# Layer 2 of a four-layer network on one core: token factors spread by TensorE, kernel weights made once at a turn's end, four patch banks, biases on ScalarE

## The chip, the core and the metric

One Trainium2 chip, of which the kernel uses one NeuronCore. Its engines run side by side and wait for each other through semaphores: TensorE (PE in the profile; its weight loads are PEld), VectorE (DVE), ScalarE (ACT), GpSimd (POOL) and SyncE (SP), whose queue issues the DMAs. SBUF is the working memory, PSUM the eight banks of 2 KB per partition that matmuls write to. The metric is the device time of one execution, in microseconds, as a median of several runs.

## The reference, cut to what matters

Four layers, each `x = x + layer(groupnorm(x))`, on 16 images of 64 x 64 tokens and 256 channels. The change lies in the end of layer 1 and in layer 2.

Layer 1 ends with a gate per token and a batch norm:

```python
xc = x * ca_gate
...
ma = xc * jax.nn.sigmoid(y)
...
sa = xc * jax.nn.sigmoid(s)
x2 = ma + sa
mean = jnp.mean(x2, axis=(0, 1, 2))
var = jnp.var(x2, axis=(0, 1, 2))
out = (x2 - mean) * lax.rsqrt(var + EPS) * bn_gamma + bn_beta
return jax.nn.relu(out)
```

The two sigmoids add up to one number per token, the token factor. Layer 2 is an involution: every token gets its own 3 x 3 kernel for each of 16 groups of 16 channels.

```python
r = jnp.einsum('bhwc,cd->bhwd', x, Wr) + br
r = jax.nn.relu((r - mean) * jax.lax.rsqrt(var + BN_EPS) * gamma + beta)
w = jnp.einsum('bhwd,dk->bhwk', r, Ws) + bs
w = w.reshape(B, H, W, G, KK)[:, :, :, :, None, :]
xi = jnp.einsum('bhwc,cf->bhwf', x, Wi) + bi
...
patches = patches.reshape(B, H, W, G, F // G, KK)
out = jnp.sum(w * patches, axis=-1)
```

Here `KK` is 9, so 144 weights per token, and one token's 256 outputs are 2304 products and their sums.

## The kernel before, in words

**Where the edited code stands.** The block that opens the pools `b_const` to `b_acc` (L826) does the end of layer 1 and the whole of layer 2. It first runs `batch_norm` (L879): 128 steps, one for each image and chunk of 512 tokens, in which TensorE spreads a row of token factors over all 128 partitions (L925: a column of the identity, broadcast, as weights, and the 128 x 512 table `held` as the moving operand) into a PSUM tile `pf`, VectorE multiplies (L933) and ScalarE squares. The results of image 0 are kept; the other images are multiplied again later.

**The pipeline of layer 2.** After that comes a loop of 148 turns (L1287 onward, `TURNS`). Four jobs run in each turn, for a chunk (image i, row chunk rc, 512 tokens) that is `LAG` = 0, 10, 18 and 28 turns behind: the end of layer 1 (`end_of_layer1`), the projection to `xi` (`projected`), the involution itself, and the centring of the result for layer 3 (`centred`). Eight turns make an image. The order of every engine's instructions is the order in which the Python code emits them (`tc.manual_schedule`); the pools decide the waits: a tile from a pool with n buffers waits for the release of the tile n allocations earlier.

One turn, in the order of the code:
- `loads(n+1)` (L1273): DMAs for the next turn, on SP's queue: `x2p`, `x2r`, and by `load_layer1` (L986) the tile `x1` (two DMAs) and the tile `pf` (two DMAs that broadcast a row of factors from DRAM over 128 partitions). Then the stores of the turn before.
- `step()` (L97) moves every running chain on by one `yield`. The chains are `norm2(i)` (L1056) and `norm3(i)` (L1237), which make the constants of a group norm over several turns; `step` is called three times a turn, at its start, in the middle (`between`) and near its end.
- `end_of_layer1` (L999): two VectorE operations (L1008), one per half of the channels, make z = (x1 - mean) * pf. The first writes a tile `z`, the second writes over `pf`. Then ScalarE's relu (L1017), GpSimd's add (L1021, x2 = z + x1), and in `between` ScalarE's squares (L1028).
- `weights(now[1], 1)` (L1124): TensorE makes the second 72 of the 144 kernel weights for 4 x 128 tokens, four products into a PSUM tile `pw` of one bank.
- `prepare` for the next chunk: `reduced2` (L1111; TensorE `pr`, ScalarE `rt`), `summed` and `evicted` (L1169, L1177) for the chunk before, and `patches` (L1134): nine groups of four transposes into a bank `pt`, each group copied out by ScalarE (L1151 `xs`). After the third group `between` runs: `weights(rt, 0)`, the squares and a `step()`.
- `residual` (L1156, `lo`), `turned` (L1201) and `statistics3`, then `projected` (L1090; TensorE `px`, ScalarE `pad`). In the turn that prepares a new image's first chunk, the projection's last chunk comes inside `patches`, before the groups that need it.
- `products(0, ...)` (L1181): VectorE multiplies patches by weights, 4608 elements per partition, from SBUF `xs` and PSUM `pw`; GpSimd sums them (L1198, L1199). `products(1, ...)` follows, whose sum VectorE makes itself (L1357).

**PSUM.** Eight banks: pool `tr` has three (for `pr`, `pt`, `px`, `pf` of the batch norm, the turned tiles and the small products of the norms, all in one rotation), `pwp` three (`pw`), `acc` two (`lo`).

**The bias.** The last step of `norm2` stands at a turn's start: after TensorE's `pm` (L1079), VectorE makes `b2` (L1085) and `bis` (L1087), ahead of that turn's z.

Of the kernel before, what the change touches and what calls it, by code (L numbers as in the profile page):

```python
# [15 lines left out]
P = 128  # L16
# [20 lines left out]
def network(ctx: ExitStack, tc: tile.TileContext, a: dict, out: bass.AP):  # L37
# [730 lines left out]
    facr = fac_d.rearrange("(i c) t -> i (c t)", i=NI)  # L768
# [57 lines left out]
    with ExitStack() as st:  # L826
# [4 lines left out]
        tr = st.enter_context(tc.tile_pool(name="b_tr", bufs=3, space=PSUM))  # L831
        pwp = st.enter_context(tc.tile_pool(name="b_pw", bufs=3, space=PSUM))
# [37 lines left out]
        loaded, stores, begun = [], [], []  # L870
        kept = {}

        def spare(pool, shape, tag):

            t = pool.tile(shape, F32, tag=tag, name="kept")
            flat = t.rearrange("p a b c -> p (a b c)")
            return flat[:, 0 : NCH * CT].rearrange("p (n h t) -> p n h t", n=NCH // 2, h=2)

        def batch_norm():  # L879
# [8 lines left out]
            held = wk.tile([P, 2, 256], F32, tag="z", name="held", bufs=1)  # L888
            held = held.rearrange("p a b -> p (a b)")[0 : NI * NCH]
# [26 lines left out]
            for k, (i, ch) in enumerate(todo):  # L916
                begin(k + 5)
                x1 = tiles.pop(k)
                pf = tr.tile([P, CT], F32, tag="tr", name="pf")
                parts = [(ch, 0, CT)]  # L920
                if not i:
                    parts = [(g * 4 + ch // 2, ch % 2 * 256, 256) for g in range(2)]
                for g, (row, c0, m) in enumerate(parts):
                    row += i * NCH
                    nc.tensor.matmul(  # L925
                        pf[:, g * m : g * m + m],
                        lhsT=ident[0 : NI * NCH, row : row + 1].broadcast_to([NI * NCH, P]),
                        rhs=held[:, c0 : c0 + m], start=True, stop=True,
                    )
                for h in range(2):  # L930
                    z = x1[:, h] if i else kept[ch][1][:, h]
                    at = slice(i * NCH + ch, i * NCH + ch + 1)
                    nc.vector.scalar_tensor_tensor(  # L933
                        z, x1[:, h], ngm1[:, i, h : h + 1], pf, ALU.add, ALU.mult,
                        accum_out=tot[:, 0, h, at],
                    )
                    sq = z if i else wk.tile([P, CT], F32, tag="sq", name="sq", bufs=1)
                    nc.scalar.activation(sq, z, AF.Square, accum_out=tot[:, 1, h, at])
# [47 lines left out]
        def load_layer1(i, rc):  # L986
            tks = [slice(g * 2048 + rc * 256, g * 2048 + rc * 256 + 256) for g in range(2)]
            load("x1", [P, 2, 2, 256], *(
                (lambda t, g=g: t[:, :, g], x1_d[i, :, :, tks[g]].rearrange("h p t -> p h t"))
                for g in range(2)  # L990
            ))
            load("pf", [P, 2, 256], *(
                (lambda t, g=g: t[:, g], facr[i, tks[g]].partition_broadcast(P)) for g in range(2)
            ))
# [4 lines left out]
        def end_of_layer1(i, rc):  # L999
# [4 lines left out]
            if i:  # L1004
                x1, pf = taken("x1"), taken("pf")
                zs = [wk.tile([P, 2, 256], F32, tag="z", name="z", bufs=1), pf]
                for h, z in enumerate(zs):
                    nc.vector.scalar_tensor_tensor(  # L1008
                        z, x1[:, h], ngm1[:, i, h : h + 1], pf, ALU.add, ALU.mult
                    )  # L1010
# [45 lines left out]
        def norm2(i):  # L1056
# [26 lines left out]
            yield  # L1083
            b2 = small.tile([64, 1], F32, tag="b2", name="b2")
            nc.vector.tensor_scalar(b2, pm[0:64, 2:3], sb2[0:64, 2:3], sb2[0:64, 1:2], ALU.mult, ALU.add)  # L1085
            bis = small.tile([P, 2], F32, tag="bis", name="bis")
            nc.vector.tensor_tensor(bis, bi, pm[:, 0:2], ALU.subtract)  # L1087
# [36 lines left out]
        def weights(rt, oh):  # L1124

            pw = pwp.tile([P, 4, 72], F32, tag="pw", name="pw")
            for r in range(4):
                nc.tensor.matmul(
                    pw[:, r], lhsT=rt[:, r * P : (r + 1) * P], rhs=ws[:, oh * 72 : oh * 72 + 72],
# [51 lines left out]
        def products(oh, pw, xs):  # L1181
            pd = pd_p.tile([P, 4, P, 9], F32, tag="pd", name="pd")
            run = xs.rearrange("p e j c -> p (e j c)")[:, oh * 9 * P : (oh + 1) * 9 * P]
            run = bass.AP(run.tensor, run.offset, [run.ap[0], [3 * C, 4], [9 * 16, 8], [9, 16], [1, 9]])
            nc.vector.tensor_tensor(  # L1185
                pd.rearrange("p r (g f) k -> p r g f k", f=16),
                run,
                pw.rearrange("p r (g k) -> p r g k", k=9).unsqueeze(3).broadcast_to(
                    [P, 4, 8, 16, 9]
                ),  # L1190
                ALU.mult,
            )
# [90 lines left out]
        with tc.manual_schedule():  # L1283
# [3 lines left out]
            for n in range(TURNS):  # L1287
# [14 lines left out]
                if inv:  # L1302
                    w1 = weights(now[1], 1)
                    x3 = wk.tile([P, 4, C], F32, tag="x3", name="x3", bufs=3)
# [7 lines left out]
                def prepare(late):  # L1312
# [7 lines left out]
                    def between():  # L1320
                        ahead.append(weights(rt, 0))
# [24 lines left out]
                if inv:  # L1346
                    pd = products(0, now[2], now[3])
# [6 lines left out]
                if inv:  # L1354
                    pd1 = products(1, w1, now[3])
                if inv:
                    nc.vector.tensor_reduce(x3[:, :, P:C], pd1, AX.X, ALU.add)  # L1357
                made = (*inv, x3, los) if inv else None
# [395 lines left out]
```

## Time and profile before

| | us |
|---|---|
| median of 3 runs | 7944.51 |
| lowest, highest | 7941.79, 7947.63 |
| profiled execution | 7971.0 |
| its span, first to last instruction | 7969.2 |
| batch statistics (first L925 to last L933) | 3164.5 to 3343.4 |
| layer 2's first and last product (L1185 starts) | 3455.9, 5599.4 |

| engine | busy us | share of the span |
|---|---|---|
| PE | 6865.4 | 86% |
| DVE | 5671.4 | 71% |
| ACT | 4934.1 | 62% |
| POOL | 3053.4 | 38% |

In the group lines of the profile, a line names the code line, the engine and operation, output and inputs, shapes, how often it ran; then busy time and mean duration in ns; then the idle time of the engine before it and who ended that. In timeline lines the first number is the start in us from the span's start and the second the duration; brackets hold idle time before. TensorE runs an fp32 matmul as two records, a transpose as one. Shares over the whole span are means over stages with different limits, so layer 2 is read by itself.

### The profile page before, as it was taken

What the parts mean: (1) busy time and instruction counts of PE and PEld (TensorE: products, weight loads), DVE (VectorE), ACT (ScalarE), POOL (GpSimd) and SP (SyncE); (2) the same over time, 40 slices, a digit from 0 to 9 for tenths busy, and PEclk for the clock granted to TensorE, in tenths of its full rate; (3) what the DMA queues carried; (4) which work ended last, traced back from release to release, by engine and by line L of the source; (5) the groups of instructions that cost most, each with busy time, mean ns of one, the idle gap of its engine ahead of it and who ended that gap; (6) DMA issues with size and microseconds to landing.
All of it is one profiled execution on the core that took longest, in us unless ns stands there. A gap on an engine that the chain in (4) does not pass through costs nothing.

```text
span 7969.2 us, 213876 instructions
## 1 busy us (share of the span) xinstructions
PE 6865.4 (86%) x88812; PEld 5137.4 (64%) x88812; DVE 5671.4 (71%) x6527; ACT 4934.1 (62%) x11456; POOL 3053.4 (38%) x2171
## 2 busy tenths in 40 slices
PE   7888888888888977689989999999788888888887
PEld 4666666666666664156666666666577777777776
DVE  6777777777777765879999999999444444444444
ACT  3555555555555554978787777776455555555554
POOL 1222222222222221168888888888222221111112
PEclk9999999999999986899999999999899999999999
DMA  7644444444443333967888888876688888888887
GB/s 216 196 149 133 138 137 133 135 135 135 134 137 112 117 103 103 327 209 264 285 282 286 270 287 275 288 265 224 209 259 260 258 255 261 256 253 258 248 257 236
DMA packets 1075308, 1689.89 MB, mean 212 GB/s; under 512 B 136273, under 2 KB 680354, under 8 KB 1073186
## 3 DMA queue, kind: packets, MB, share of 16 engines
q1 hardware_dynamic: 1074338, 1676.21, 65.4%
q8 instruction: 700, 11.47, 0.6%
q14 instruction: 270, 2.21, 0.1%
HBM read 1228.85 MB, written 469.76 MB: 213 GB/s over the span
## 4 chain that ended last, share of the span: by engine, by line
PE 46%; DVE 23%; issue 12%; ACT 8%; DMA 7%; POOL 3%; SPq 1%; DVEq 0%; POOLq 0%; ACTq 0%
PE pk L1458 13%; DVE pd L1185 9%; PE pa L1524 8%; PE pkv L270 5%; PE py L412 5%; DMA xn<-in_x 2%; PE pq L258 2%; PE pr L1425 2%; DVE x L1357 2%; PE pctx L336 2%; PE px L1097 1%; DVE mq L371 1%; ACT sq L421 1%; DVE z L1008 1%; DVE mq L378 1%
## 5 line engine op out<-in xcount | busy, mean ns | idle before, releaser
L1185 DVE TENSOR_TENSOR pd<-xs,pw 128x4608 f32<-128x4608 f32 x256 | 1256.0, 4947 | 5.5 <-POOL x L1199 5.3
L1458 PE MATMUL pk<-rt,span 64*128 64x176 f32 x12288 | 1183.6, 329 | 61.2 <-issue 55.0
L1468 ACT ACTIVATE wm<-pk,spanb 128x176 f32<-128x176 f32 x2560 | 845.8, 425 | 574.3 <-PE pk L1458 572.5
L1544 POOL TENSOR_TENSOR ex<-ex,rx 128x192 f32<-128x192 f32 (+2 forms) x768 | 436.7, 570 | 1826.5 <-DVE ex L1537 1329.4
L1198 POOL TENSOR_TENSOR pd<-pd 128x2048 f32<-128x2048 f32 (+2 forms) x384 | 1072.2, 2792 | 88.5 <-DVE pd L1185 68.4
L1458 PEld LDWEIGHTS pk<-rt,span 64*128 64x128 f32 x12288 | 973.2, 192 | 139.0 <-issue 81.3
L1537 DVE SCALAR_TENSOR_TENSOR ex<-pa,msk,ex 128x192 f32<-128x192 f32 x704 | 294.2, 418 | 1019.2 <-ACT ex L1536 951.9
L270 PE MATMUL pkv<-wq,xn 128*128 128x256 f32 x4096 | 979.3, 385 | 3.6 <-ACT va L279 2.0
L1524 PE MATMUL pa<-wm,xw 126*32 126x48 f32 x45056 | 751.1, 214 | 213.8 <-issue 201.0
L1473 DVE TENSOR_TENSOR wm<-pk,spanb 128x704 f32<-128x704 f32 x896 | 794.0, 888 | 192.0 <-PE pk L1458 188.8
L270 PEld LDWEIGHTS pkv<-wq,xn 128*128 128x128 f32 x4096 | 782.1, 194 | 229.3 <-issue 116.4
L366 POOL TENSOR_TENSOR qa<-qa,mq 128x1024 f32<-128x1024 f32 x256 | 501.5, 1980 | 1027.3 <-DVE mq L371 514.2
L1524 PEld LDWEIGHTS pa<-wm,xw 126*32 126x32 f32 x45056 | 620.8, 111 | 396.1 <-issue 352.0
L1147 PE MATMUL pt<-ident,pad 128*128 128x128 f32 x4608 | 604.6, 280 | 146.0 <-ACT xs L1151 122.7
L1147 PEld LDWEIGHTS pt<-ident,pad 128*128 128x128 f32 x4608 | 505.3, 142 | 294.1 <-ACT xs L1151 145.9
L1357 DVE TENSOR_REDUCE x<-pd 128x512 f32<-128x4608 f32 x128 | 634.0, 4953 | 4.4
L412 PE MATMUL py<-wo,o 128*128 128x256 f32 x2048 | 542.5, 422 | 64.8 <-ACT va L279 59.7
L1151 ACT COPY xs<-pt 128x512 f32<-128x512 f32 x1152 | 584.4, 597 | 17.5 <-PE pt L1147 17.4
L258 PE MATMUL pq<-xn,wq 128*128 128x512 f32 x1024 | 539.7, 644 | 34.1 <-ACT xn L133 21.6
L412 PEld LDWEIGHTS py<-wo,o 128*128 128x128 f32 x2048 | 496.2, 310 | 110.2 <-ACT va L279 76.9
L1536 ACT ACTIVATE ex<-pa,msk 128x192 f32<-128x192 f32 x704 | 299.7, 426 | 389.6 <-PE pa L1524 179.7
L1097 PE MATMUL px<-x2p,wis 128*128 128x512 f32 x1024 | 477.5, 610 | 46.1 <-ACT xs L1151 36.9
(243 smaller groups left out, 11780.3 us busy)
## 6 DMA issues: line engine op xcount, KB each, us to landing
xw<-strips SPq DMA_DIRECT2D x1408, 256.0 KB
xn<-in_x SPq DMA_DIRECT2D x256, 512.0 KB
x_d<-x SPq DMA_DIRECT2D x256, 512.0 KB
strips<-cen SPq DMA_DIRECT2D x352, 256.0 KB
xin<-in_x SPq DMA_DIRECT2D x128, 512.0 KB
x<-in_x SPq DMA_DIRECT2D x128, 512.0 KB
xm<-x_d SPq DMA_DIRECT2D x128, 512.0 KB
x2p<-x_d SPq DMA_DIRECT2D x128, 512.0 KB
```

The costliest lines, as they stand in the source:

```text
L258: nc.tensor.matmul(pq, lhsT=wq[:, h, f0 : f0 + P], rhs=xn[:, h], start=(h == 0), stop=(h == 1),)
L270: nc.tensor.matmul(pkv[:, q], lhsT=xn[:, h, q * P : (q + 1) * P], rhs=wq[:, h, f0 + P : f0 + 384], start=(h == 0), stop=(h == 1),)
L412: nc.tensor.matmul(py[:, q, :], lhsT=om[i, hf][:, :, ch * 4 + q], rhs=wo[:, hf, :], start=(hf == 0), stop=(hf == 1),)
L1147: nc.tensor.transpose(pt[:, k, h * P : (h + 1) * P], lines[:, h, rc * 4 + e + k, 2 * j : 2 * j + P], ident,)
L1151: nc.scalar.copy(xs[:, e : e + 2, j, :], pt)
L1185: nc.vector.tensor_tensor(pd.rearrange("p r (g f) k -> p r g f k", f=16), run, pw.rearrange("p r (g k) -> p r g k", k=9).unsqueeze(3).broa ...
L1198: nc.gpsimd.tensor_tensor(pd[..., 0:n], pd[..., 0:n], pd[..., n : 2 * n], ALU.add)
L1357: nc.vector.tensor_reduce(x3[:, :, P:C], pd1, AX.X, ALU.add)
L1458: nc.tensor.matmul(pkv[:, b, m], lhsT=span[half, first + gg, s0 : s0 + P], rhs=rto[half, o // 4 * 2 + m, :], start=True, stop=True,)
L1468: nc.scalar.activation(dst[:, m // 2, m % 2], pkv[:, m // 2, m % 2], AF.Identity, bias=spanb[:, g0 + m : g0 + m + 1],)
L1473: nc.vector.tensor_tensor(dst, pkv, spanb[:, g0 : g0 + 4].rearrange("p (b m) -> p b m", b=2).unsqueeze(3).broadcast_to([P, 2, 2, NTL]), AL ...
L1524: nc.tensor.matmul(pav[p0 : p0 + 32, :, tj * TC : (tj + 1) * TC].rearrange("c g (w v) -> c g w v", v=2), lhsT=xw[0:TILE_IN, k, tj, 32 * q ...
```

## The change

1. The token factor of the loop's turns is no longer loaded. The table `held` becomes a constant of the block; a function `factors` does what L925 did, into a `tr` bank, and is called at the end of every turn for the next turn's chunk. The two z operations read that bank and write both halves of one tile `z`.
2. All 144 kernel weights of a chunk are made by four products (instead of eight of half the width), at the end of the turn before the one that uses them, into one tile `pw` of two banks, of which there is one.
3. Because a tile now lies in two banks, each `products` call multiplies in two instructions of 2304 elements.
4. The pool `tr` gets four banks, `pwp` two (one tile), `acc` two as before.
5. `b2` and `bis` are made by ScalarE, in three instructions, one `yield` later.

```diff
-        tr = st.enter_context(tc.tile_pool(name="b_tr", bufs=3, space=PSUM))
-        pwp = st.enter_context(tc.tile_pool(name="b_pw", bufs=3, space=PSUM))
+        tr = st.enter_context(tc.tile_pool(name="b_tr", bufs=4, space=PSUM))
+        pwp = st.enter_context(tc.tile_pool(name="b_pw", bufs=1, space=PSUM))
...
+        held = bconst("held", [NI * NCH, CT])
+
+        def factors(i, parts):
+
+            pf = tr.tile([P, CT], F32, tag="tr", name="pf")
+            for g, (row, c0, m) in enumerate(parts):
+                row += i * NCH
+                nc.tensor.matmul(
+                    pf[:, g * m : g * m + m],
+                    lhsT=ident[0 : NI * NCH, row : row + 1].broadcast_to([NI * NCH, P]),
+                    rhs=held[:, c0 : c0 + m], start=True, stop=True,
+                )
+            return pf
+
+        def both_halves(rc):
+            return [(g * 4 + rc // 2, rc % 2 * 256, 256) for g in range(2)]
...
-            load("pf", [P, 2, 256], *(
-                (lambda t, g=g: t[:, g], facr[i, tks[g]].partition_broadcast(P)) for g in range(2)
-            ))
...
             if i:
-                x1, pf = taken("x1"), taken("pf")
-                zs = [wk.tile([P, 2, 256], F32, tag="z", name="z", bufs=1), pf]
-                for h, z in enumerate(zs):
+                x1, pf = taken("x1"), spread.pop()
+                z = wk.tile([P, 2, 2, 256], F32, tag="z", name="z", bufs=1)
+                zs = [z[:, h] for h in range(2)]
+                for h in range(2):
                     nc.vector.scalar_tensor_tensor(
-                        z, x1[:, h], ngm1[:, i, h : h + 1], pf, ALU.add, ALU.mult
+                        zs[h], x1[:, h], ngm1[:, i, h : h + 1],
+                        pf.rearrange("p (g t) -> p g t", g=2), ALU.add, ALU.mult,
                     )
...
             yield
+            yield
             b2 = small.tile([64, 1], F32, tag="b2", name="b2")
-            nc.vector.tensor_scalar(b2, pm[0:64, 2:3], sb2[0:64, 2:3], sb2[0:64, 1:2], ALU.mult, ALU.add)
+            nc.scalar.activation(
+                b2, pm[0:64, 2:3], AF.Identity, bias=sb2[0:64, 1:2], scale=sb2[0:64, 2:3]
+            )
             bis = small.tile([P, 2], F32, tag="bis", name="bis")
-            nc.vector.tensor_tensor(bis, bi, pm[:, 0:2], ALU.subtract)
+            for h in range(2):
+                nc.scalar.activation(
+                    bis[:, h : h + 1], pm[:, h : h + 1], AF.Identity,
+                    bias=bi[:, h : h + 1], scale=-1.0,
+                )
...
-        def weights(rt, oh):
+        def weights(rt):
 
-            pw = pwp.tile([P, 4, 72], F32, tag="pw", name="pw")
+            pw = pwp.tile([P, 2, CT], F32, tag="pw", name="pw")
+            pw = pw[:, :, 0:288].rearrange("p b (o r k) -> p b o r k", o=2, r=2)
             for r in range(4):
                 nc.tensor.matmul(
-                    pw[:, r], lhsT=rt[:, r * P : (r + 1) * P], rhs=ws[:, oh * 72 : oh * 72 + 72],
+                    pw[:, r // 2, :, r % 2], lhsT=rt[:, r * P : (r + 1) * P], rhs=ws.rearrange("p (o k) -> p o k", o=2),
                     start=True, stop=True,
                 )
             return pw
...
-            run = bass.AP(run.tensor, run.offset, [run.ap[0], [3 * C, 4], [9 * 16, 8], [9, 16], [1, 9]])
-            nc.vector.tensor_tensor(
...
+            for b in range(2):
+                part = bass.AP(
+                    run.tensor, run.offset + b * 6 * C,
+                    [run.ap[0], [3 * C, 2], [9 * 16, 8], [9, 16], [1, 9]],
+                )
+                nc.vector.tensor_tensor(
+                    pd[:, 2 * b : 2 * b + 2].rearrange("p r (g f) k -> p r g f k", f=16),
+                    part,
+                    pw[:, b, oh].rearrange("p r (g k) -> p r g k", k=9).unsqueeze(3).broadcast_to(
+                        [P, 2, 8, 16, 9]
+                    ),
+                    ALU.mult,
+                )
...
                 if inv:
-                    w1 = weights(now[1], 1)
                     x3 = wk.tile([P, 4, C], F32, tag="x3", name="x3", bufs=3)
...
                     def between():
-                        ahead.append(weights(rt, 0))
                         if squares:
...
+                    pd1 = products(1, now[1], now[2])
                     nc.vector.tensor_reduce(x3[:, :, P:C], pd1, AX.X, ALU.add)
+                if nxt:
+                    ahead[1] = weights(ahead[1])
+                after = jobs(n + 1)[0]
+                if after and after[0]:
+                    spread.append(factors(after[0], both_halves(after[1])))
```

Built, the changed kernel has on each engine the order that this code gives. In TensorE's queue a turn ends with `px`, then `pm` or `pg` of a norm where there is one, then `pw` (its first product waits for VectorE), `pf`, and the next turn's `pr`. On VectorE the first z waits for TensorE as well as for the two DMAs of `x1` and for GpSimd. On ScalarE `b2` and `bis` stand after the squares, between the third and the fourth copy to `xs`.

More of the change, by code (lines that the diff above doesn't have):

```diff
@@ L767, in network @@
     maps_st.close()
-    facr = fac_d.rearrange("(i c) t -> i (c t)", i=NI)
     def folded(pool, name, mean, var, gamma, beta, shift):
@@ L869, in network @@
         st0, st3, gn2, ngm2 = {}, {}, {}, {}
-        loaded, stores, begun = [], [], []
+        loaded, stores, begun, spread = [], [], [], []
         kept = {}
@@ L887, in batch_norm @@
             tot = wk.tile([P, 2, 2, NI * NCH], F32, tag="c3", name="tot")
-            held = wk.tile([P, 2, 256], F32, tag="z", name="held", bufs=1)
-            held = held.rearrange("p a b -> p (a b)")[0 : NI * NCH]
             nc.sync.dma_start(out=held, in_=fac_d)
@@ L918, in batch_norm @@
                 x1 = tiles.pop(k)
[L919 to L929, printed above, removed]
+                pf = factors(i, [(ch, 0, CT)] if i else both_halves(ch))
                 for h in range(2):
@@ L1183, in products @@
             run = xs.rearrange("p e j c -> p (e j c)")[:, oh * 9 * P : (oh + 1) * 9 * P]
-            run = bass.AP(run.tensor, run.offset, [run.ap[0], [3 * C, 4], [9 * 16, 8], [9, 16], [1, 9]])
[L1185 to L1192, printed above, removed]
+            for b in range(2):
[11 more added lines that the diff above has]
+                )
             return pd
@@ L1346, in network @@
                 if inv:
-                    pd = products(0, now[2], now[3])
+                    pd = products(0, now[1], now[2])
                     sums_on_pool(pd, x3)
@@ L1354, in network @@
                 if inv:
-                    pd1 = products(1, w1, now[3])
-                if inv:
+                    pd1 = products(1, now[1], now[2])
                     nc.vector.tensor_reduce(x3[:, :, P:C], pd1, AX.X, ALU.add)
+                if nxt:
[3 more added lines that the diff above has]
+                    spread.append(factors(after[0], both_halves(after[1])))
                 made = (*inv, x3, los) if inv else None
```

## The prediction

> **What bounds the kernel now.** I read the slices first (where each engine is full), then the groups of instructions of layer 2, then one turn of layer 2 engine by engine in the timeline, and last the turns in which that rhythm breaks.
>
> Busy tenths in 40 slices of 199 us:
>
> ```profile
> PE   7888888888888977689989999999788888888887
> DVE  6777777777777765879999999999444444444444
> ACT  3555555555555554978787777776455555555554
> ```
>
> The edited code runs in slices 16 to 28 (3166 to 5620 us). From 3456 us on DVE (VectorE) stands at nine tenths there, PE (TensorE) too, but its busy time is modelled. What DVE does, with mean ns and idle time before it:
>
> ```profile
> L1185 DVE TENSOR_TENSOR pd<-xs,pw 128x4608 f32<-128x4608 f32 x256 | 1256.0, 4947 | 5.5 <-POOL x L1199 5.3
> L1357 DVE TENSOR_REDUCE x<-pd 128x512 f32<-128x4608 f32 x128 | 634.0, 4953 | 4.4
> L933 DVE SCALAR_TENSOR_TENSOR x<-x,ngm,pf 128x512 f32<-128x512 f32 x240 | 162.6, 744 | 5.6 <-DMA x<-x_d 4.3 <-PE pf L925 0.4 <-ACT x L938 0.4
> L1008 DVE SCALAR_TENSOR_TENSOR z<-x,ngm,pf 128x512 f32<-128x512 f32 x120 | 118.5, 988 | 60.5 <-DMA pf<-fac_d 58.9 <-issue 0.4
> L1008 DVE SCALAR_TENSOR_TENSOR pf<-x,ngm,pf 128x512 f32<-128x512 f32 x120 | 90.2, 752 | 4.3
> L1085 DVE TENSOR_SCALAR b<-pm,sb 64x1 f32<-64x1 f32 x16 | 4.3, 270 | 53.9 <-PE pm L1079 53.9
> ```
>
> Almost no idle time stands before the big ones. To be seen: the same z operation takes 752 ns in one half and 988 in the other. The timeline of a plain turn says why (start, duration):
>
> ```profile
> 4615.90 1.64 POOL L1199 TENSOR_TENSOR x<-pd 128x512 f32<-128x512 f32 x1
> 4616.86 1.22 DVE L1008 SCALAR_TENSOR_TENSOR z<-x,ngm,pf 128x512 f32<-128x512 f32 x1
> 4618.12 0.75 DVE L1008 SCALAR_TENSOR_TENSOR pf<-x,ngm,pf 128x512 f32<-128x512 f32 x1
> 4618.79 9.81 DVE L1185 TENSOR_TENSOR pd<-xs,pw 128x4608 f32<-128x4608 f32 x2
> 4628.63 4.95 DVE L1357 TENSOR_REDUCE x<-pd 128x512 f32<-128x4608 f32 x1
> ```
>
> The first z ends 0.54 us after POOL's sum x (4617.54), as if it began only then; where POOL has finished, it takes 0.73 to 0.77. Start to start the turn is 1.26 + 0.67 + 9.84 + 4.87 = 16.64 us, all DVE. TensorE in the same turn:
>
> ```profile
> 4624.97 1.63 PE L1147 MATMUL pt<-ident,pad 128*128 128x128 f32 x12 [1.38 <-ACT xs L1151]
> 4626.44 1.04 PE L1163 MATMUL lo<-ident,x2r 128*128 128x128 f32 x8
> 4627.31 1.04 PE L1209 MATMUL pt<-ident,x 128*128 128x128 f32 x8
> 4628.19 3.60 PE L1097 MATMUL px<-x2p,wis 128*128 128x512 f32 x8
> 4631.62 1.01 PE L1128 MATMUL pw<-ws,rt 65*128 65x72 f32 x8
> 4632.56 1.93 PE L1118 MATMUL pr<-x2r,wrs 128*64 128x512 f32 x4
> ```
>
> It has one hole, 1.38 us before the last transposes, and is otherwise full: a second loop almost as long as DVE's. The rhythm breaks once per image of eight turns, where the first operation of a turn is the bias of the next image:
>
> ```profile
> 4538.78 5.29 PE L1097 MATMUL px<-x2p,wis 128*128 128x512 f32 x8 [2.65 <-ACT xs L1151]
> 4545.19 1.53 PE L1147 MATMUL pt<-ident,pad 128*128 128x128 f32 x12 [1.12 <-ACT pad L1108]
> 4549.62 0.27 DVE L1085 TENSOR_SCALAR b<-pm,sb 64x1 f32<-64x1 f32 x1 [3.50 <-PE pm L1079]
> ```
>
> DVE waits because TensorE is late: px waited for a bank, and in 4538.70 to 4540.00 its granted clock was 0.50.
>
> **The change, part by part** (us; negative is gained).
>
> 1. Products in halves: 256 instructions of 4608 elements become 512 of 2304. Two products back to back last 9.81 in all with 4.947 each, so the second starts 4.863 after the first: 4608 elements at 0.96 per ns (4.80) and 0.063 per instruction. Two more per turn: +0.126. The dear end is the whole duration, 0.147 over the elements plus the 0.03 before a dependent start, per added instruction: +0.35. I take +0.13, since the halves depend on nothing between them, as in the row; the difference, 0.22 x 128 = 29, stays for the range. A gain is excluded: the elements are the same.
>    [...]
>
> 2. z from PSUM. L933 is this operation with a PSUM factor: 744 ns, shown with POOL idle. Beside POOL no row shows it; the products, which also read one SBUF tensor and one PSUM tensor, keep 4947 all the time that POOL adds beside them, so I take 0.67 start to start for both halves. Ends: 0.67 and the 1.26 of today. A plain turn on DVE becomes 0.67 + 0.67 + 9.97 + 4.87 = 16.18, against 16.64.
>
> 3. TensorE's turn. Out: 16 records of pw (0.117 apart, 1.87). In: 8 records of 144 columns, between the 0.117 of 72 columns and the 0.12 of the 128-column transposes on one side, twice 0.117 on the other; px runs 512 columns in 0.43, 0.84 ns a column, so 0.12 to 0.13, nearest the low end: 1.04. And the factors: four records of 256 columns, shown in the batch statistics (L925, 4 in 1.10). They are a new wait for z, and behind z on DVE stand products and reduce, behind it on ACT the relus, then POOL. So the loop z, ACT, PE, z has to be added up. From the first relu: ACT starts its fourth xs copy 6.23 later; with three banks pt's seventh group waits for it, with four the eighth does: 6.85, then two groups 0.98, lo 0.87, turned x 0.88, px 3.43, pw 1.04, factors 1.10 = 15.15, and z with its hand-over 0.85: 16.0. DVE's 16.18 still rules, by 0.2. I take 16.2. The other wait, pw on the end of the products (one buffer instead of three), is met: they end 10.5 after the relu, pw starts at 13.0; behind it wait factors, pr and all of the next turn.
>
> 4. The transition turn. The bias leaves DVE (0.26 a time, two instructions) and ACT gets three small ones, 0.2 to 0.3 each by its 128x64 row (0.33), one step later, when pm is long done. But the wait does not go: z now needs the factors, which stand behind pm and pw. With four banks the first px needs an earlier copy: 5.75 after the relu, the second 8.1, no clock drop; pad copies to 11.1, transposes, lo, turned and pm to 15.4, pw and factors 17.55, z 18.4 after the previous z. Before: 18.43 in a typical image (3844.84 to 3863.27), 20.03 at 4549.88. Ends: 16.2 and 20.0; I take 18.4. The extra ACT work makes the next PE loop 16.6, under the 17.5 which that turn lasts anyway for its moments.
>
> 5. An image: before, by z starts from 3844.84 to 3981.26, 18.43 + 17.53 + 16.52 + 16.31 + 16.67 + 16.63 + 16.64 + 17.69 = 136.4; the mean of 109 turns (3454.47 to 5315.86) gives 136.6. After: 18.4 + 17.55 + 16.5 + 4 x 16.2 + 17.25 = 134.5. So -2.1 x 13.6 images = -28.
>
> 6. Loads. 240 DMAs of pf go, 0.9 of SP issue and 256 KB a turn. In the full pipeline this is worth nothing: DVE never waits for data there, and x1 is issued a turn ahead. In the ramp (3376 to 3437) a turn lasts 6.5, and z waits on pf (58.9 in all): the chain load, z, relu, POOL's add, next load spans two turns and holds two issues of 0.45 and half a MB. About 1 a turn: -8, between 0 and -14. Then the factors come from PE, which is idle there.
>
> 7. The tail has no z. 18 turns of 15.34, paced by product and POOL: +0.13 each, less one bias wait of 1.6: +1.
>
> 8. Batch statistics: four banks change nothing, DVE and ACT are full there (39 of 40 us). Layers 0, 1, 3: untouched.
>
> Sum: -28 - 8 + 1 = -35. The profiled execution took 7971.0 (span 7969.2), the median of the runs shown is 7944.5, 26.5 less; I take the difference to the median: 7909. About 0.2% (16 us) is what a measurement can tell here.
>
> **The rivals.**
> A, the sum as it stands, 0.55: 7909, own range 7895 to 7925.
> B, the halves cost their full overhead, 0.12: +29, 7938, no difference that can be told. For it: a wait between them. Against: the 9.81.
> C, slower, 0.15: the new factor wait makes the PE loop the bound. It has only 0.2 of slack against the new DVE turn and 0.64 against the old. Should pw's split output or hand-overs cost 1.0 more, a turn is 17.0 and the image 17.0 x 4 + 17.3 + 17.6 + 17.3 + 19.4 = 139.6: +3 x 13.6 - 7 = +34, 7978. It decides from a loop of about 16.8. For it: PE is 90% full. Against: every matmul has a row at its own or a near size.
> D, z is not freed: POOL holds it back with a PSUM factor too, 0.06: 0.24 (988 less 744) x 109 = +26, 7935.
> E, TensorE catches up and the transition loses its wait, 0.12: -2.2 x 13.6 = -30, 7880.
>
> Faster 0.68 (A, E and a little of D), within 0.2% 0.16 (B, most of D), slower 0.16 (C). Range 7878 to 7952: it holds A, B, D and E and leaves out C.
>
> **What would show it.** Products of 2.55, four in about 10.0; first z at 0.74 beside POOL's x; plain turns of 16.2 with no DVE idle. z waiting on PE pf only in transitions, about 2 each; px there at 3.6 and clock 1.00; ramp turns of 5.5. Wrong if plain turns show z waiting for pf (C), or four products take 10.3 (B).

## The result and the profile after

The changed kernel takes 7897.57 us (median of four runs, 7892.94 to 7903.11) against 7946.07 for the kernel before beside it (7941.79 to 7972.13). The ratio is 0.9936, 95% interval 0.9916 to 0.9955: 36 to 67 us faster. The forecast was 7909, its range 7878 to 7952. The profiled execution took 7902.17, its span is 7900.4.

Where the time went, from the two timelines. The marks are starts of DVE operations: `gsum` (L854 before, L853 after) begins the batch statistics, and the last `ab` ahead of the loop (L967, L971) ends them.

| stretch | before | after | difference | forecast |
|---|---|---|---|---|
| batch statistics | 198.2 | 199.1 | +0.9 | 0 |
| ramp: from there to the z ahead of the first product | 104.7 | 92.0 | -12.7 | -8 |
| loop: from that z to the last z, 109 turns | 1861.4 | 1825.7 | -35.7 | -28 |
| tail: from there to the last reduce | 288.6 | 289.1 | +0.5 | +1 |
| sum | 2452.9 | 2405.9 | -47.0 | -35 |

The two profiled spans differ by 68.8, more than layer 2. Of the rest, 17.9 lie behind layer 2 and 3.9 ahead of it, in code that is the same in both. A second profile of the changed kernel had 2334.4 behind layer 2 where this one had 2346.9, so that part changes from execution to execution, and only the stretches above are set against the forecast.

The groups of VectorE (DVE) after; the columns are as in the profile before:

```profile
L1200 DVE TENSOR_TENSOR pd<-xs,pw 128x2304 f32<-128x2304 f32 x512 | 1272.6, 2548 | 5.8 <-POOL x L1214 5.4
L1369 DVE TENSOR_REDUCE x<-pd 128x512 f32<-128x4608 f32 x128 | 634.0, 4953 | 4.4
L1010 DVE SCALAR_TENSOR_TENSOR z<-x,ngm,pf 128x512 f32<-128x512 f32 x240 | 168.1, 742 | 99.9 <-PE pf L885 51.7 <-DMA x<-x_d 40.7 <-POOL x L1024 6.7
```

Both z operations are now one group with one duration, 742 ns; the 988 of the first half is gone. DVE's timeline of a plain turn, GpSimd (POOL) and TensorE beside it:

```profile
4454.27 4.95 DVE L1369 TENSOR_REDUCE x<-pd 128x512 f32<-128x4608 f32 x1
4458.15 1.65 POOL L1214 TENSOR_TENSOR x<-pd 128x512 f32<-128x512 f32 x1
4459.14 1.40 DVE L1010 SCALAR_TENSOR_TENSOR z<-x,ngm,pf 128x512 f32<-128x512 f32 x2
4460.45 9.94 DVE L1200 TENSOR_TENSOR pd<-xs,pw 128x2304 f32<-128x2304 f32 x4
...
4472.93 1.15 PE L1139 MATMUL pw<-ws,rt 65*128 65x144 f32 x8
4473.91 1.03 PE L885 MATMUL pf<-held,ident 128*128 128x256 f32 x4
4475.30 1.40 DVE L1010 SCALAR_TENSOR_TENSOR z<-x,ngm,pf 128x512 f32<-128x512 f32 x2
```

To be seen: POOL's sum x runs to 4459.80, and z starts in the middle of it and takes its ordinary time. From z to z it is 16.16 (16.64 before), and there is no idle time on DVE. The spread factor pf ends at 4474.94, 0.36 ahead of the z that reads it. In the transition turns, where the products of a new image begin, it comes too late:

```profile
4498.12 1.98 PE L1107 MATMUL px<-x2p,wis 128*128 128x512 f32 x4
4501.42 1.98 PE L1107 MATMUL px<-x2p,wis 128*128 128x512 f32 x4 [1.32 <-ACT xs L1162]
4504.52 1.53 PE L1158 MATMUL pt<-ident,pad 128*128 128x128 f32 x12 [1.13 <-ACT pad L1118]
4511.05 1.41 DVE L1010 SCALAR_TENSOR_TENSOR z<-x,ngm,pf 128x512 f32<-128x512 f32 x2 [2.29 <-PE pf L885]
```

DVE waits 2.29 for pf; z to z it is 18.54. The px products have full clock here (1.00 granted in 4498 to 4506). The kernel before had two kinds of such turns. In ten of the loop's thirteen full transitions px took 3.70 and DVE waited 1.9 for pm, as in this one:

```profile
4686.06 0.27 DVE L1085 TENSOR_SCALAR b<-pm,sb 64x1 f32<-64x1 f32 x1 [1.91 <-PE pm L1079]
```

In the other three px took 5.25 to 6.72, with a granted clock down to 0.50, and the wait was 3.45 to 4.91; the one that the prediction shows (3.50) is of these.

### The profile page after: what moved, and what is told of

It is laid out like the page before. It is cut to its first block, busy times and chain, and to the rows that moved or that the text cites. A ratio compares the mean times of both kernels' runs of the same rounds, so it can differ in the third digit from the quotient of the medians.

```text
span 7900.4 us, 212578 instructions
## 1 busy us (share of the span) xinstructions
PE 6841.6 (87%) x88268; PEld 5101.3 (65%) x88268; DVE 5640.1 (71%) x6751; ACT 4944.2 (63%) x11504; POOL 3053.7 (39%) x2171
## 5 line engine op out<-in xcount | busy, mean ns | idle before, releaser
L1200 DVE TENSOR_TENSOR pd<-xs,pw 128x2304 f32<-128x2304 f32 x512 | 1272.6, 2548 | 5.8 <-POOL x L1214 5.4
L1158 PE MATMUL pt<-ident,pad 128*128 128x128 f32 x4608 | 563.1, 276 | 141.1 <-ACT xs L1162 102.6
```

The lines of the kernel that those rows point to most:

```text
L1158: nc.tensor.transpose(pt[:, k, h * P : (h + 1) * P], lines[:, h, rc * 4 + e + k, 2 * j : 2 * j + P], ident,)
L1200: nc.vector.tensor_tensor(pd[:, 2 * b : 2 * b + 2].rearrange("p r (g f) k -> p r g f k", f=16), part, pw[:, b, oh].rearrange("p r (g k) -> ...
```

## Experiments

The runs were made in three sets, each with its own runs of the kernel before. For all of them the same thing was read from the trace: from the start of one reduce to the start of the next, a mean over twelve images for each turn of an image. "Transition" is the turn whose products are the first of the next image, with its z; "next" is the turn behind it. Between the two and after them lie plain turns; the seventh, with the moments, hardly changes.

| kernel | next | 2nd | plain (four) | 7th | transition | image | ratio to the kernel before |
|---|---|---|---|---|---|---|---|
| before | 17.51 | 16.63 | 16.64 | 17.29 | 18.79 | 136.8 | 1 |
| halves alone (e1) | 17.52 | 16.68 | 16.65 | 17.27 | 18.68 | 136.7 | 1.0002 (0.9988 to 1.0015) |
| banks alone (e2) | 17.50 | 17.70 | 16.73 | 17.55 | 19.71 | 139.4 | 1.0047 (1.0031 to 1.0063) |
| changed (e0) | 17.36 | 16.49 | 16.16 | 17.21 | 18.54 | 134.2 | 0.9923 (0.9900 to 0.9947) |
| three banks (e5) | 17.83 | 17.05 | 16.60 | 17.21 | 21.83 | 140.3 | 1.0042 (1.0032 to 1.0052) |
| factor loaded (e6) | 17.55 | 16.66 | 16.64 | 17.30 | 16.65 | 134.7 | 0.9953 (0.9936 to 0.9969) |
| biases on DVE (e7) | 17.32 | 16.49 | 16.16 | 17.21 | 18.54 | 134.2 | 0.9934 (0.9917 to 0.9952) |
| factors first (e3) | 17.34 | 16.49 | 16.16 | 17.24 | 17.56 | 133.3 | 0.9913 (0.9896 to 0.9929) |
| factor copied to SBUF (e4) | 17.40 | 16.74 | 16.69 | 17.21 | 18.27 | 136.4 | 0.9995 (0.9985 to 1.0005) |
| whole products (e8) | 17.89 | 17.32 | 16.87 | 17.22 | 19.38 | 139.3 | 1.0029 (1.0016 to 1.0041) |
| factor ahead of pm (e9) | 17.81 | 16.49 | 16.16 | 17.15 | 17.26 | 133.3 | 0.9913 (0.9898 to 0.9927) |

The 18.79 of the kernel before is 18.4 in ten of the twelve images and 20.0 and 21.4 in the two whose px had the lower clock.

**The changed kernel again (e0)**, beside e5, e6 and e8.

> The changed kernel itself, beside the others of this batch. Every theory: ratio 0.991 to 0.996 to the kernel before; plain turn 16.16, transition z to z 18.54, last layer-2 stretch from the z before the first product to the last z 1825.7 within 1.

The ratio is 0.9923 and the loop 1825.6, 0.1 from the first profile. The loop repeats within 0.3 us where a kernel was run twice (here, and e3 and e10), so differences of some microseconds between traces can be read there. The ramp repeats within 1.2.

**Products in halves, alone (e1).** The kernel before, with two products of 2304 elements in place of each of 4608:

```diff
-            run = bass.AP(run.tensor, run.offset, [run.ap[0], [3 * C, 4], [9 * 16, 8], [9, 16], [1, 9]])
-            nc.vector.tensor_tensor(
...
+            for b in range(2):
+                part = bass.AP(
+                    run.tensor, run.offset + b * 6 * C,
+                    [run.ap[0], [3 * C, 2], [9 * 16, 8], [9, 16], [1, 9]],
+                )
...
+                    pw[:, 2 * b : 2 * b + 2].rearrange("p r (g k) -> p r g k", k=9).unsqueeze(3).broadcast_to(
```

> The kernel before with one part of the change alone: each product in two halves. Additive theory (the halves cost 0.13 us of DVE a turn, and the turn is all DVE): plain turn 16.65 + 0.13 = 16.78, z unchanged at 1.2 in its first half, in all about +16 us. Rival (port loop: the first z cannot run before POOL's sum x has ended, so z, relu, POOL's adds and sums, 16.1, and 0.54 of z set the turn): plain turn stays at 16.65, the first z shrinks by 0.13 to about 1.1, only the turns in which z is not held back grow, in all about +8 us.

Four products take 9.94, 0.13 more than two whole ones, as the prediction had it. But the turn stays at 16.65. The timeline of DVE, POOL and ACT in a plain turn of this run:

```profile
4450.84 1.28 POOL L1021 TENSOR_TENSOR x<-z,x 128x512 f32<-128x512 f32 x1 [1.57 <-ACT z L1017]
4452.07 1.28 POOL L1021 TENSOR_TENSOR x<-pf,x 128x512 f32<-128x512 f32 x1
4453.31 2.39 POOL L807 TENSOR_TENSOR cen<-xc,gmb 128x1024 f32<-128x1024 f32 x1
4455.67 8.52 POOL L1202 TENSOR_TENSOR pd<-pd 128x2048 f32<-128x2048 f32 x3
4460.50 4.95 DVE L1361 TENSOR_REDUCE x<-pd 128x512 f32<-128x4608 f32 x1
4464.27 1.65 POOL L1203 TENSOR_TENSOR x<-pd 128x512 f32<-128x512 f32 x1
4465.37 1.10 DVE L1008 SCALAR_TENSOR_TENSOR z<-x,ngm,pf 128x512 f32<-128x512 f32 x1
4466.50 0.75 DVE L1008 SCALAR_TENSOR_TENSOR pf<-x,ngm,pf 128x512 f32<-128x512 f32 x1
4466.50 0.81 ACT L1017 ACTIVATE z<-z,bnp,ab 128x512 f32<-128x512 f32 x1 [2.26 <-DVE z L1008]
4467.17 9.94 DVE L1189 TENSOR_TENSOR pd<-xs,pw 128x2304 f32<-128x2304 f32 x4
4467.49 1.28 POOL L1021 TENSOR_TENSOR x<-z,x 128x512 f32<-128x512 f32 x1 [1.57 <-ACT z L1017]
```

The first z became shorter, from 1.22 to 1.10. It ends 0.55 after POOL's x, which ends at 4465.92; the same stands in the plain turns of this run and of the kernel before (0.53 to 0.56). A port, which the expectations of this run, of e6 and of e8 name as the cause, is shown by no run: what they show is this time. POOL works from its first add to x almost without idle time and then waits 1.57 for ACT's relu of z. So the kernel before was not held by DVE's own work alone: a loop z, ACT's relu, POOL's two adds, its centring, its sums, x, and back to z set 16.64. DVE's added work was taken out of the waiting that hides in z's duration. The expectation's +8 us for the turns in which z isn't held do not show: the loop is 1860.2, 1861.4 before.

**Four banks, alone (e2).** The kernel before with four `tr` banks; of the eight PSUM banks (3, 3 and 2 in the kernel before) two, not three, are then left for the weights:

```diff
-        tr = st.enter_context(tc.tile_pool(name="b_tr", bufs=3, space=PSUM))
-        pwp = st.enter_context(tc.tile_pool(name="b_pw", bufs=3, space=PSUM))
+        tr = st.enter_context(tc.tile_pool(name="b_tr", bufs=4, space=PSUM))
+        pwp = st.enter_context(tc.tile_pool(name="b_pw", bufs=2, space=PSUM))
```

> The kernel before with four tr banks and two pw buffers, nothing else. If the transition is late because px waits for a bank: px follows the sixth group within about 0.5, its clock stays at 1.00, the last three groups begin about 11.2 after the relu (14.5 before), DVE's wait for pm falls from 2.3 on average to under 0.5, some -25 us in all; plain turns stay at 16.65. If the transition is late for another reason (the pad copies, the x2p load): waits of 2 stay, within 8 us of the kernel before.

A miss, and no clean test. It is slower. TensorE's waits in the loop are no longer for the copies to xs, which are down to 0.8 us, but for the products that free a weight tile:

```profile
PE pw L1128 <- DVE pd L1185: 147.9, 101, 2.5
PE pt L1147 <- ACT pad L1108: 14.7, 13, 1.1
```

(From: waiting line, releaser; total us, times, longest.) The granted clock fell as well: its mean over 3455 to 5315 is 0.96, against 1.00 in the kernel before. In the loop's transitions px no longer waits for a bank, but it took 3.60 to 5.16, so the clock of 1.00 that was expected held in five of thirteen only. How much of the loss is the clock's and how much the wait's, no run tells. As long as `lo` keeps two banks, the fourth bank for `tr` costs the weights one of their three. What it is worth is read from the next run.

**Three banks in the changed kernel (e5).**

```diff
-        tr = st.enter_context(tc.tile_pool(name="b_tr", bufs=4, space=PSUM))
+        tr = st.enter_context(tc.tile_pool(name="b_tr", bufs=3, space=PSUM))
```

> The changed kernel with three rotating PSUM banks instead of four for the patch transposes, px, pr and pf; everything else is kept. Theory 'the fourth bank is needed' (pf is one more tile in the rotation, so with three banks a group of transposes or a projection waits for a copy that ScalarE does one step later): plain turn 16.16 to 16.3, transition z to z 18.54 to about 21.9 (the second px waits for the last patch copy behind ScalarE's wrs and wis), together about 54 us slower than the changed kernel. Rival 'the bank is spare': plain turn and transition within 0.1 of the changed kernel's, within 5 us in all.

The loop grew by 80.8 (1825.6 to 1906.4), more than expected; the whole is slower than the kernel before. The transition is 21.83, near the 21.9 expected. TensorE and DVE in one of them:

```profile
4677.12 5.40 PE L1107 MATMUL px<-x2p,wis 128*128 128x512 f32 x8 [2.65 <-ACT xs L1162]
4683.64 1.53 PE L1158 MATMUL pt<-ident,pad 128*128 128x128 f32 x12 [1.12 <-ACT pad L1118]
4689.05 1.03 PE L885 MATMUL pf<-held,ident 128*128 128x256 f32 x4
4690.17 1.41 DVE L1010 SCALAR_TENSOR_TENSOR z<-x,ngm,pf 128x512 f32<-128x512 f32 x2 [5.70 <-PE pf L885]
```

The busy time by stretch of the same run, where the third number from the end is TensorE's granted clock:

```profile
4678.00:4679.00 1.00, 1.00 (x2) 0.38 (x2) 1.00 (x1) 0.03 (x1) 1.00 (x1) 0.50 1.01 357
4679.00:4680.00 1.00, 1.00 (x2) 0.33 (x1) 0.96 (x2) 0.00 (x0) 0.92 (x2) 0.50 0.33 116
```

All of px waits 2.65 for the fourth copy to xs and then runs at a granted clock of 0.50: 5.40 in place of 3.60. The expectation had the wait and not the clock. In the one image where px took 3.70 after the same wait (4538.52) the transition is 20.25, so some 1.6 of the 21.83 are the clock's and the agreement is in part luck. The plain turn missed: 16.60 for 16.3. Here z waits 0.35 for pf in every plain turn, so this is TensorE's loop. The prediction had it at 16.0 with four banks, and 6.85 less 6.23 = 0.62 longer with three: 16.6. The expectation had not used the prediction's own term.

**The factor loaded again (e6).** The changed kernel, with pf read by two DMAs a chunk into SBUF, as before the change; its core:

```diff
+            load("pf", [P, 2, 256], *(
+                (lambda t, g=g: t[:, g], facr[i, tks[g]].partition_broadcast(P)) for g in range(2)
+            ))
...
-                x1, pf = taken("x1"), spread.pop()
-                z = wk.tile([P, 2, 2, 256], F32, tag="z", name="z", bufs=1)
...
+                x1, pf = taken("x1"), taken("pf")
+                zs = [wk.tile([P, 2, 256], F32, tag="z", name="z", bufs=1), pf]
...
-                after = jobs(n + 1)[0]
-                if after and after[0]:
-                    spread.append(factors(after[0], both_halves(after[1])))
```

> The changed kernel with the token factor loaded into SBUF by two broadcast DMAs a chunk as in the kernel before, z with both inputs from SBUF; the four half products, the weights at a turn's end, four banks and the biases on ScalarE are kept. Theory 'loop through the shared port' (z with two SBUF inputs starts only when GpSimd's sums of the same turn are done, and takes 1.1 or more): plain turn back to 16.65, no wait of VectorE on the spread factor in the transition (z to z 16.7 to 17.0 there), ramp 8 to 12 us longer; together about +18 us against the changed kernel, ratio 0.994 to 0.998 to the kernel before. Rival 'only where the weights and the factor stand in TensorE's queue matters, the input of z does not': plain turn 16.16 and transitions shorter by 1.3 to 2.3 each, about -25 us against the changed kernel.

The plain turn is back at 16.64, and the transition is only 16.65. From the end of the batch statistics to the last z it is 1932.2 against 1918.1 in e0: 14.1 longer, 18 expected. Of this, 5.3 lie ahead of the first product (99.1 against 93.8), where 8 to 12 were expected: in the ramp of e6 z waits for the DMA of pf ten times, 67.0 in all. The rest is the image, 134.7 against 134.2: what the PSUM factor gains in plain turns it gives back, all but 0.5, in the transition. Of the 2.6 an image that the whole change gains over the kernel before, 2.1 come without it. By the medians of the set the difference is 27, the traces show 14.

**Factors ahead of the weights (e3).** The changed kernel with two calls exchanged:

```diff
-                if nxt:
-                    ahead[1] = weights(ahead[1])
                 after = jobs(n + 1)[0]
                 if after and after[0]:
                     spread.append(factors(after[0], both_halves(after[1])))
+                if nxt:
+                    ahead[1] = weights(ahead[1])
```

> The changed kernel with the factors ahead of the weights in TensorE's queue. If the wait of 2.29 in the transition is TensorE's tail pm, pw, pf: it falls by pw's 1.0 to about 1.25, 14 times, -15 us against the changed kernel; plain turns stay at 16.16, since they do not wait. Rival: the wait only moves from z to the products, which need pw: no gain. (pw should be ready 1.2 after z starts, the products start 1.32 after it.)

The wait in the transition falls from 2.29 to 1.31:

```profile
4493.60 1.41 DVE L1010 SCALAR_TENSOR_TENSOR z<-x,ngm,pf 128x512 f32<-128x512 f32 x2 [1.31 <-PE pf L885]
```

The loop is 1812.9, 12.7 less than the changed kernel's, 15 expected. No other run has a shorter loop; by the time of the whole kernel it can't be told from the changed one (0.9913 and 0.9923, with intervals that overlap). It was run once more in another set (e10), and the ratio was 0.9908 (0.9890 to 0.9927).

> The kernel of e3_factors_first again, beside the two others. Every theory: ratio to the kernel before 0.989 to 0.993, transition 17.56, the stretch from the z before the first product to the last z 1812.9 within 1.

In that run the loop is 1813.1 and the transition 17.55.

**The factor from TensorE, but in SBUF (e4).** The kernel of e3, with ScalarE copying the spread factor to SBUF, so that nothing is loaded and z has two SBUF inputs as in the kernel before:

```diff
-                z = wk.tile([P, 2, 2, 256], F32, tag="z", name="z", bufs=1)
-                zs = [z[:, h] for h in range(2)]
...
+                zs = [wk.tile([P, 2, 256], F32, tag="z", name="z", bufs=1), pf]
...
-                    spread.append(factors(after[0], both_halves(after[1])))
+                    spun = factors(after[0], both_halves(after[1]))
+                    spread.append(wk.tile([P, 2, 256], F32, tag="pf", name="pf", bufs=1))
+                    nc.scalar.copy(spread[-1], spun.rearrange("p (g t) -> p g t", g=2))
```

> As e3_factors_first, but ScalarE copies the factor from PSUM into SBUF and both z operations read it there, as the kernel before did, so nothing is loaded and z has two SBUF inputs again. If it is POOL's sum beside it that holds z back: first z about 1.2 again, plain turn 16.6, about +25 to +30 us against e3_factors_first. If z was slow for the load or for anything else that the change took away: z stays at 0.75, plain turn 16.2, within 8 us of e3.

The loop grows by 43.6 to 1856.5, more than the 25 to 30 expected (the transition, where z now waits for the copy, is 0.7 longer too). The plain turn is 16.69, and z behaves as in the kernel before:

```profile
4455.15 1.64 POOL L1212 TENSOR_TENSOR x<-pd 128x512 f32<-128x512 f32 x1
4456.23 1.11 DVE L1009 SCALAR_TENSOR_TENSOR z<-x,ngm,pf 128x512 f32<-128x512 f32 x1
```

x ends at 4456.79 and z at 4457.34, 0.55 later, as in e1. There are no loads here, and yet the plain turn is lost. With e6 this settles what made the plain turn shorter: that z has one SBUF input, not that the loads are gone. Why two SBUF inputs should hold it no run shows. The durations beside POOL's x are 742 ns with one SBUF input (735 to 749 in the changed kernel's loop) and 1.03 to 1.39 us with two in the plain turns of e1, e4, e6 and the kernel before.

**Whole products (e8).** The kernel of e3 with one product of 4608 elements for each half again; for that the weights are two tiles of one bank, made by eight products of 72 columns:

```diff
-        pwp = st.enter_context(tc.tile_pool(name="b_pw", bufs=1, space=PSUM))
+        pwp = st.enter_context(tc.tile_pool(name="b_pw", bufs=2, space=PSUM))
...
-                    pw[:, r // 2, :, r % 2], lhsT=rt[:, r * P : (r + 1) * P], rhs=ws.rearrange("p (o k) -> p o k", o=2),
+                    pw[:, r], lhsT=rt[:, r * P : (r + 1) * P], rhs=ws[:, oh * 72 : oh * 72 + 72],
...
-                    ahead[1] = weights(ahead[1])
+                    ahead[1] = [weights(ahead[1], oh) for oh in range(2)]
```

> The kernel with the factors ahead of the weights (e3_factors_first), but each half's product in one instruction again, the weights as two tiles of one bank with 72 columns a pass, two buffers, both after the factor. Theory 'with z free of the port VectorE's own work is the plain turn, and each instruction's fixed part counts': plain turn 16.15 to 16.03, the stretch from the first to the last z 14 us shorter than with e3_factors_first, about 2 us less in the tail, ratio 0.989. Rival 'TensorE carries the turn': eight passes of 72 columns take 1.87 and not 0.98, the weights come later, plain turn 16.16 or longer, no gain or up to 20 us slower than e3_factors_first.

The rival holds, at four times its price: the loop is 1893.0, 80 more than e3. A plain turn of this run:

```profile
4456.67 4.95 DVE L1364 TENSOR_REDUCE x<-pd 128x512 f32<-128x4608 f32 x1
4461.26 1.03 PE L885 MATMUL pf<-held,ident 128*128 128x256 f32 x4
4462.12 1.91 PE L1138 MATMUL pw<-ws,rt 65*128 65x72 f32 x16
4462.38 1.41 DVE L1010 SCALAR_TENSOR_TENSOR z<-x,ngm,pf 128x512 f32<-128x512 f32 x2 [0.75 <-POOL x L1209]
4463.96 1.93 PE L1128 MATMUL pr<-x2r,wrs 128*64 128x512 f32 x4
```

z now waits 0.75. The profile names POOL's x, which ends at 4462.37 here; in the changed kernel z starts in the middle of that operation, so the wait is read as pf's, which ends at 4462.29 and was 0.1 ahead of z in e3's transition as well; for some 40 other waits of z in this loop the profile names pf itself. The turn of 16.87 fits TensorE's loop: the 16.0 of the prediction, and 0.86 for weights that take 1.84 start to start in place of 0.98. The eight products of the kernel before were hidden beside a turn of 16.64; they would not be beside this one.

**The biases on VectorE (e7).**

```diff
-            yield
...
-            nc.scalar.activation(
-                b2, pm[0:64, 2:3], AF.Identity, bias=sb2[0:64, 1:2], scale=sb2[0:64, 2:3]
-            )
+            nc.vector.tensor_scalar(b2, pm[0:64, 2:3], sb2[0:64, 2:3], sb2[0:64, 1:2], ALU.mult, ALU.add)
...
+            nc.vector.tensor_tensor(bis, bi, pm[:, 0:2], ALU.subtract)
```

> The changed kernel with the two biases on VectorE again, one step earlier as before; everything else is kept. Theory 'the biases are beside other work on either engine' (they fall into VectorE's wait for the spread factor in the transition): stretch from the z before the first product to the last z within 3 us of the changed kernel's 1825.6. Rival 'on VectorE they wait for the products with wis in front of the products': plus 0.26 to 2.7 an image, 4 to 35 us longer.

The loop is 1825.4, against 1825.6: nothing, as long as z waits for pf behind pm. The wait is only shared out anew:

```profile
4500.83 0.27 DVE L1088 TENSOR_SCALAR b<-pm,sb 64x1 f32<-64x1 f32 x1 [0.20 <-PE pm L1082]
4501.03 0.14 DVE L1090 TENSOR_TENSOR bis<-bi,pm 128x2 f32<-128x2 f32 x1
4502.93 1.41 DVE L1010 SCALAR_TENSOR_TENSOR z<-x,ngm,pf 128x512 f32<-128x512 f32 x2 [1.76 <-issue]
```

0.20, the two biases and 1.76 make up the 2.29 that the changed kernel waits for pf.

**The factor ahead of pm too (e9).** The kernel of e3 with the call of `factors` in front of the step that issues the products pm:

```diff
                     sums_on_pool(pd, x3)
+                after = jobs(n + 1)[0]
+                if after and after[0]:
+                    spread.append(factors(after[0], both_halves(after[1])))
                 step()
...
-                after = jobs(n + 1)[0]
-                if after and after[0]:
-                    spread.append(factors(after[0], both_halves(after[1])))
```

> The kernel with the factors ahead of the weights, the factors moved once more, ahead of the step that issues the twelve one-column products with wis and wrs (1.27 us of TensorE in the transition turn); the weights stay behind these. Theory 'in the transition TensorE's queue is now the bound, so the weights end last': z's wait of 1.31 goes, but the products, which begin 0.5 after the weights' last pass in e3_factors_first, then wait for the weights, so the transition goes from 17.56 to 17.1 or 17.2 and the stretch from the z before the first product to the last z is 5 us shorter. Rival 'z alone holds the transition': 17.56 to 16.3, 16 us shorter. A second rival, 'the factor's bank is now taken earlier than the one before it comes free': plain turns longer by 0.1 or more, 10 us longer.

z no longer waits in the transition, but the products behind it do, 0.92:

```profile
4499.85 1.41 DVE L1010 SCALAR_TENSOR_TENSOR z<-x,ngm,pf 128x512 f32<-128x512 f32 x2
4500.80 1.25 PE L1139 MATMUL pw<-ws,rt 65*128 65x144 f32 x8
4502.18 9.95 DVE L1200 TENSOR_TENSOR pd<-xs,pw 128x2304 f32<-128x2304 f32 x4 [0.92 <-ACT z L1020]
```

They start 0.13 after the last pw ends (4502.05), so the wait is read as pw's, though the profile names ACT. The transition is 17.26 (17.1 to 17.2 expected), but the next turn rises from 17.34 to 17.81, where the moments now stand behind pf and DVE waits 0.8 for pg. The image is the same 133.3, and the loop 1815.1 against 1812.9 and 1813.1: no gain. In the transition and the turn behind it TensorE's queue is the bound, and an exchange inside it only moves the wait.

## Why the prediction was right

The likeliest case, A, came out: 7897.57 lies in its own range of 7895 to 7925, and the sum of layer 2 was -35 against -47.0 measured: the mechanism of the changed kernel's plain turn held, and two terms, the image and the ramp, were too small. By its steps:

1. Halves: 9.97 for four start to start forecast, 9.94 + 0.03 measured. In the changed kernel this term stands in the turn of 16.16, so +0.13 was right, and rival B is excluded. The forecast's rate of 0.96 elements a ns is what the two pages give: 4947 ns for 4608 elements before, 2548 for 2304 after, so 2399 for the 2304 between. Between independent products back to back these runs show 0.13. e1 adds what the prediction missed: in the kernel before the same step costs nothing.
2. z: forecast 0.67 each, plain turn 16.18; measured 16.16. Rival D is excluded, since z keeps 742 ns beside POOL. The cause, given as a likeness to the products, is shown by e4 and e6.
3. TensorE's loop: 16.0 forecast. In plain turns pf comes 0.36 ahead of z, of which about 0.1 is the hand-over that the transitions show (pf ends at 4510.96 in the one above, z starts at 4511.05), so the loop is about 15.9. pw takes 0.98 start to start (1.04 forecast). Rival C did not come, but e5 and e8 show it: with TensorE's loop longer by 0.6 or 0.9 the plain turn was 16.60 and 16.87, and both kernels were slower than the one before (in e5 by the transition as well). Its price was about right too: an image of 139.6 forecast at a loop of 17.0, 139.3 measured at 16.87.
4. Transition: 18.4 forecast, 18.54 measured. pad's transposes were put at 11.1 after the relu; they start 11.2 after it. Rival E is excluded, but e6 shows how near it lay: with all of the change but the spread factor the transition has 16.65, against 18.79 before, and the factor in TensorE's queue puts 1.9 of this back. Against a transition of the kernel before at full clock (18.4, px in 3.70) the changed kernel's is no shorter; what it gained there in these profiles, 0.25 in the mean, is that none of its transitions fell to the lower clock (no px record of its loop takes over 0.70, against up to 1.22 before). That px would keep its clock was forecast.
5. Image: -2.1 forecast. By the loop's time over its 109 turns it was 136.6 before and is 134.0 after, -2.6: this term of the sum was too small, by 7.7 in all. Of the 0.5, the forecast for the turn behind the transition was 0.2 too long (17.55; 17.36) and for each plain turn 0.04, the transition 0.14 too short. The first and the last, incomplete images make up the rest.
6. Ramp: -8 forecast, -12.7 measured, inside the bounds of 0 and -14. The turns went from 6.5 to 5.1, not to 5.5. e6, where z waits for the loads and the turns last 6.1, puts 5.3 on them (one execution of each kernel); the other part isn't explained by any run. e1, with the loads and all the rest of before, was itself 3.0 shorter than before there, so part of it is spread between executions. Taking the loads away is not enough by itself: in e4, where z waits for ScalarE's copy instead, it is 101.1 to the first product, against 99.1 in e6.
7. Tail: +1 forecast, +0.5 measured.
8. Batch statistics: 0 forecast, +0.9 measured. The biases on ScalarE, part of step 4, are worth nothing beside the spread factor (e7); without it no run tells.

What the prediction did not see is that "all DVE" was not what held the plain turn before. It counted 1.26 start to start for the first z as DVE's own time. e1 shows that this time was elastic, with a loop over POOL behind it. With 0.67 for it DVE's own work was 16.05 before, and the change made it longer, 16.18, while the turn became shorter. The sum came out because the change took z out of that loop, so that DVE's work then did set the turn; that the turn of the kernel before was entered as measured, and not worked out, kept the error out of the difference.

## What to carry to other kernels

Where an instruction's duration differs between two places with the same shape, its long form can hold a wait (here the first z, 1.22 us in a plain turn and 0.73 to 0.77 where x had ended before it): ask which loop ends in it before adding or taking away work around it, for the work may cost or gain nothing. Add up the second loop before freeing the first: here TensorE had less than 0.3 us of slack in a plain turn, and one PSUM bank less (e5) or eight narrow matmuls in place of four wide ones (e8) turned some 50 us less than before into 25 to 35 us more, in e5 more than half of it in the transitions. In a queue, put first what is waited for first, but in a turn where that queue is itself the bound, an exchange only moves the wait.

## What the runs showed of the hardware that was not expected

- VectorE's z with two SBUF inputs ended 0.53 to 0.57 us after GpSimd's x in the plain turns of e1, e4, e6 and the kernel before, at durations from 1.03 to 1.39 us; where x had ended before it began, it takes 0.73 to 0.78. By these two numbers some 0.2 of it lie ahead of the point at which it is held, an estimate (0.75 less 0.55).
- An fp32 product on TensorE of 144 columns costs 0.122 us a pass (the changed kernel's pw, eight in 0.98 start to start), one of 72 columns 0.115 (e8, sixteen in 1.84): twice the columns at hardly more time.
- TensorE's granted clock went to 0.50 after a pause of 2.65 us (e5) and stayed there over some 3 us, but the same pause did not always do it: px behind it took 5.09 to 6.77 in 13 of e5's 14 transitions and 3.70 in one, and 3.70 in ten of thirteen of the kernel before. Two pauses of 1.32 and 1.13, with 1.98 of work between them, left it at 1.00 (the changed kernel, 4498 to 4506). In e2, where no wait of TensorE in the loop exceeds 2.5, its mean is 0.96.
